# Gated cross-attention with a mixture of biases on one core: the mask's bias added by VectorE, in the operation that takes each head's maximum

## The chip, the core and the metric

The program runs on one core of a Trainium2 chip. A core has engines with queues of their own, which run side by side and wait for each other through semaphores: TensorE (PE in the profile; PEld is its loading of weights), VectorE (DVE), ScalarE (ACT), GpSimd (POOL) and the DMA queue of SyncE (SP). Each engine takes its instructions strictly in the order in which they were issued. TensorE writes its results to PSUM, a small memory of eight banks, from which VectorE and ScalarE fetch them; everything else lies in SBUF.

The metric is the device time of one execution in microseconds (us), as the median of several runs.

## The reference, cut to what matters

There are B = 8 sequences of D = 512 channels and S = 2048 positions. The attention works in patches of W = 128 positions, with H = 8 heads of dh = 32 channels. The mask is one number per position; a key whose mask isn't positive gets a score of -1e9.

```python
q = einsum('ed,bdw->bew', Wq, qp) + bq[:, None]        # qp: layernorm(x), in patches
k = einsum('ed,bdw->bew', Wk, qp) + bk[:, None]
val = einsum('ed,bdw->bew', Wv, vp) + bv[:, None]      # vp: the context, in patches
scores = einsum('bhdi,bhdj->bhij', qh, kh) / sqrt(dh)
scores = where(mp[:, :, None, :] > 0, scores, -1e9)
attn = softmax(scores, axis=-1)
o = gelu(einsum('bhij,bhdj->bhdi', attn, vh))
x = x + tanh(g_xattn) * (einsum('de,bew->bdw', Wo, o) + bo[:, None]) * masks
# then a router over 64 biases: softmax, the 8 largest weights w of each channel's row
x = x + tanh(g_ffn) * (layernorm(x) * sum(w) + w @ expert_bias)
```

## The kernel before, in words

Everything is fp32. The work is cut into 32 chunks of 512 positions (four to a sequence), and each chunk into two pairs of patches, so there are 64 pairs, called `g`. A pair has 16 score matrices of 128 x 128: two patches `i`, and eight heads, numbered by `e` (two halves of the channels) and `r` (four row groups of 32 channels).

The order of the work is written out by hand. The main loop runs over `g` from 0 to 61, and the last two pairs follow with an order of their own. An iteration holds, on each engine's queue, in this order:

- `scores(g)`: TensorE computes the 16 score matrices into four PSUM banks `sc0` to `sc3`, one per row group `r`. For each bank it first issues a product of `negw` with `mneg`, in bf16, which fills the bank with the mask's bias (-1e9 as a sum of three bf16 terms where a key is masked, else 0); the scores are then added onto it in PSUM. Each `sc[r]` is 128 x 512: patch `i`, half `e`, key.
- `weigh(g-2)`: the product of the turned attention weights with the values; ScalarE copies it out (`weighed`).
- `maxima(g, ...)`: VectorE takes the negated maximum of each score row, one `tensor_reduce` of 128 x 512 per bank.
- `exps(g, q)`: ScalarE takes 16 exponentials of 128 x 128 out of PSUM, each with the negated maximum as its bias and the row's sum as a second result. `divide` takes the reciprocals of the sums (VectorE) and multiplies (GpSimd). The weights are turned by TensorE in the next iteration (`turn`), copied by ScalarE (`turned`).
- In an even iteration, from the fifth on: `attend` for two of the four output tiles of a chunk, m = 2 and 3. Its products `po` are emptied by VectorE (L541) and added to the residual by GpSimd (L544). In an odd one: `logits`, whose product `pl` VectorE adds to `lgT` (L591, or L589 for the first of a sequence).
- `queries_and_keys(g // 2 + 1, ...)`: half of the next chunk's queries and keys, by Strassen's scheme in seven block products on TensorE (L374), emptied by VectorE (L381 to L401) with two sums on GpSimd. `between` puts transposes of TensorE between the blocks.
- Statistics of later rows (VectorE), values of the next chunk (`values`, `values_out`), in odd iterations the other two `attend` tiles, and last, from g = 12 on, `mix`: two products `pb`, each added to the output tile by VectorE (L703), which is then stored.

What decides the order between engines around the change is two things. One is VectorE's queue: `maxima` of pair `g` stands behind the two L703 of the iteration before, and ahead of L541 (even) or L591 (odd) and of all that empties the block products. The other is the PSUM banks. `po`, `pl`, `pb` and the block products all take turns in two banks (`ps_mm`, tag `mm`), so each of them can start only when VectorE has emptied the product two before it. In an even iteration the first block product takes the bank that the first `po` has left; in an odd one the third block product (they come two to a bank) takes the bank that `pl` has left. The score banks have one buffer each and are also used by `values` (bank 0) and by the odd `attend` (banks 1 and 2).

The mask's row for a chunk is made by `mask(ch)`, in the middle of each even iteration: `m01` (1/sqrt(dh) for a valid key, 0 for a masked one), which also scales the keys (L401), and `mneg` (1 for a masked key).

Of the kernel before, what the change touches and what calls it, by code (L numbers as in the profile page):

```python
# [8 lines left out]

F32 = mybir.dt.float32  # L10
BF16 = mybir.dt.bfloat16
# [10 lines left out]
def bf16_terms(value, n):  # L22

    import ml_dtypes

    terms = []
    for _ in range(n):
        t = float(ml_dtypes.bfloat16(value))
        terms.append(t)
        value -= t  # L30
    assert value == 0.0
    return terms


@with_exitstack
def flamingo_gated_kernel(
# [23 lines left out]
    nc = tc.nc  # L60
# [37 lines left out]
    raw, xn, cxs, mks, xr = {}, {}, {}, {}, {}  # L98
# [93 lines left out]
    nc.vector.memset(ones, 1.0 / S)  # L192


    negw = const.tile([P, P], BF16, name="negw")
    nc.vector.memset(negw, 0.0)
    terms = bf16_terms(NEG, 3)
    for r in range(HR):
        for i in reversed(range(3)):
            nc.vector.memset(negw[r * DH : r * DH + i + 1, :], terms[i])  # L200

    d1, d2 = slice(0, NM // 2), slice(NM // 2, NM)
# [54 lines left out]
    def statistics(b, m, piece, x_):  # L260

        if b not in st1:
            st1[b] = small.tile([P, NM, S // 512, 6], F32, tag="st1", name=f"st1_{b}")
        nc.vector.bn_stats(st1[b][:, m, piece, :], x_)  # L264
# [41 lines left out]
            nc.gpsimd.tensor_tensor(t4, t2, b21, ALU.subtract)  # L306


    qss, kss, vTs, m01s, mnegs = {}, {}, {}, {}, {}
# [14 lines left out]
    def product(shape, name, r=None):  # L324

        if late:
            late.append(late.pop(0))
            r = late[0]
        if r is not None:
            return ps_sc.tile(shape, F32, tag=f"sc{r}", name=name)  # L330
        return ps_mm.tile(shape, F32, tag="mm", name=name)

    def first_queries_and_keys():


# [90 lines left out]
    def scores(g):  # L426


        ch, h = g // NH, g % NH
        sc = [ps_sc.tile([P, NPP, NE, W], F32, tag=f"sc{r}", name=f"sc_{g}_{r}") for r in range(HR)]  # L430
        rows = [slice(r * DH, (r + 1) * DH) for r in range(HR)]
        bias = mnegs[ch][:, h * HW : (h + 1) * HW].rearrange("p (a w) -> p a w", w=W)
        for r in range(HR):
            nc.tensor.matmul(  # L434
                sc[r], negw[rows[r], :],
                bias[rows[r], :, None, :].to_broadcast([DH, NPP, NE, W]),
                start=True, stop=False,
            )
        for i in range(NPP):
            ws = slice(h * HW + i * W, h * HW + (i + 1) * W)  # L440
            for e in range(NE):
                for r in range(HR):
                    nc.tensor.matmul(  # L443
                        sc[r][:, i, e, :], qss[ch][rows[r], e, ws], kss[ch][rows[r], e, ws],
                        start=False, stop=(i == NPP - 1 and e == NE - 1),
                    )
        nmx = small.tile([P, HR, NPP, NE], F32, tag="nmx", name=f"nmx_{g}")
        at = [work.tile([P, H, W], F32, tag="at", name=f"at_{g}_{i}", bufs=4) for i in range(NPP)]
        rsum = small.tile([P, NPP, H], F32, tag="rsum", name=f"rsum_{g}")
        pairs[g] = {"sc": sc, "nmx": nmx, "at": at, "rsum": rsum, "atT": {}}  # L450

    def maxima(g, rs):
        p = pairs[g]
        for r in rs:
            nc.vector.tensor_reduce(p["nmx"][:, r, :, :], p["sc"][r], AX.X, ALU.max, negate=True)  # L455
# [12 lines left out]

    def divide(g, i, engine=None):
# [276 lines left out]
    for m in range(NM):  # L746
        for j in range(NCH):
            statistics(0, m, j, xr[j][:, m, :])
        ln1[0] = aggregate(st1[0], S // 512, "1_0", m, m + 1)
        shares_of_mean(0, slice(m, m + 1))  # L750
        norm(0, (m,))
        norm(1, (m,))
        if m == NM - 1:
            mask(0)
            weight_sums()
            values_out(0, 0)
            values_out(0, 1)
            values_out(1, 0)
        next(projections)
    st1.pop(0)  # L760
    for k in range(3):
        sums_of_x(1, k)
# [27 lines left out]
    for g in range(NG - NH):  # L790
        ch, h = g // NH, g % NH
        even = h == 0
        nxt = ch + 1
# [138 lines left out]
        if fin == 2:  # L932
            nmean, rs = aggregate(st2.pop(b4), NCH, f"2_{b4}")
# [54 lines left out]
    g = h0 + 1  # L988
# [166 lines left out]
```

## Time and profile before

| what | us |
|---|---|
| median of 3 runs | 1334.58 (1334.14 to 1335.98) |
| the profiled execution | 1334.19 |
| its span | 1332.4 |
| TensorE busy | 1303.9 |
| VectorE busy | 887.1 |
| ScalarE busy | 837.1 |
| GpSimd busy | 794.3 |

"Busy" is the time in which an engine's instructions run; the span is what the profiler saw, some 2 us less than the time of the execution. TensorE's granted clock was 0.997 of full speed. The engine table alone doesn't tell what a change is worth; that is read from the chain of work that ended last, and from the timeline around the change. In the timeline each line has a start, a duration, the engine, the line of the kernel, the operation, output and input tiles, a count, and in brackets how long the engine sat idle before and what ended that. Instructions of one engine overlap a little in the records: the distance from one start to the next is what an instruction costs in its queue, and its duration is somewhat longer.

### The profile page before, as it was taken

What the parts mean: (1) busy time and instruction counts of PE and PEld (TensorE: products, weight loads), DVE (VectorE), ACT (ScalarE), POOL (GpSimd) and SP (SyncE); (2) the same over time, 40 slices, a digit from 0 to 9 for tenths busy, and PEclk for the clock granted to TensorE, in tenths of its full rate; (3) what the DMA queues carried; (4) which work ended last, traced back from release to release, by engine and by line L of the source; (5) the groups of instructions that cost most, each with busy time, mean ns of one, the idle gap of its engine ahead of it and who ended that gap; (6) DMA issues with size and microseconds to landing.
All of it is one profiled execution on the core that took longest, in us unless ns stands there. A gap on an engine that the chain in (4) does not pass through costs nothing.

```text
span 1332.4 us, 26505 instructions
## 1 busy us (share of the span) xinstructions
PE 1303.9 (98%) x9802; PEld 951.6 (71%) x9802; DVE 887.1 (67%) x1815; ACT 837.1 (63%) x2843; POOL 794.3 (60%) x802
## 2 busy tenths in 40 slices
PE   7999999999999999999999999999999999999997
PEld 4777777777777777777777777777777777777653
DVE  5776666576666766677666776667766675666656
ACT  2766765675765765756666665666755666656653
POOL 3655556575566655567655666656566665666642
PEclk9999999999999999999999999999999999999999
DMA  8434223243543443453443453434443423432214
GB/s 282 126 102 126 72 100 128 103 143 101 155 157 120 158 134 104 151 167 124 154 124 115 151 165 118 161 105 130 155 160 120 164 64 112 135 120 79 80 65 174
DMA packets 109729, 173.32 MB, mean 130 GB/s; under 512 B 9248, under 2 KB 43680, under 8 KB 109472
## 3 DMA queue, kind: packets, MB, share of 16 engines
q1 hardware_dynamic: 107536, 168.75, 39.3%
q10 hardware_dynamic: 2064, 2.88, 0.6%
q8 instruction: 77, 1.26, 0.4%
q14 instruction: 52, 0.43, 0.1%
HBM read 138.06 MB, written 33.55 MB: 129 GB/s over the span
## 4 chain that ended last, share of the span: by engine, by line
PE 92%; DVE 3%; DMA 2%; ACT 1%; issue 1%; POOL 0%; SPq 0%; DVEq 0%; ACTq 0%
PE qk L374 27%; PE po L535 17%; PE pv L411 15%; PE pt L487 8%; PE pa L506 5%; PE pb L692 5%; PE pl L573 4%; PE sc L443 4%; PE px L559 4%; PE sc L434 2%; ACT at L464 1%; PE pf L340 1%; DVE st L264 1%; DMA cx<-in_ctx 1%; DVE st L554 1%; PE pg L603 1%
## 5 line engine op out<-in xcount | busy, mean ns | idle before, releaser
L473 POOL TENSOR_TENSOR at<-at,rsum 128x1024 f32<-128x1024 f32 x128 | 244.5, 1910 | 283.3 <-DVE rsum L472 265.6
L464 ACT ACTIVATE at<-sc,nmx 128x128 f32<-128x128 f32 x1024 | 365.7, 415 | 6.0 <-DVE nmx L455 6.0
L464 ACT ACTIVATION_READ_ACCUMULATOR at<-sc,nmx 128x1 f32 x1024 | 260.7, 255 | 0.0
L411 PE MATMUL pv<-wv_sb,cx 128*128 128x256 f32 x1024 | 239.4, 383 | 6.8 <-DMA cx<-in_ctx 6.8
L535 PE MATMUL po<-o,wo_sb 128*128 128x512 f32 x512 | 234.0, 599 | 0.0
L544 POOL TENSOR_TENSOR xr<-t,xr 128x512 f32<-128x512 f32 x124 | 160.5, 1295 | 87.7 <-DVE t L541 86.6
L411 PEld LDWEIGHTS pv<-wv_sb,cx 128*128 128x128 f32 x1024 | 189.4, 192 | 29.3 <-DMA cx<-in_ctx 6.8
L516 ACT COPY o<-pa 128x512 f32<-128x512 f32 x64 | 37.5, 586 | 258.8 <-PE pa L506 258.8
L493 ACT COPY atT<-pt 128x512 f32<-128x512 f32 x256 | 151.6, 623 | 57.2 <-PE pt L487 57.0
L455 DVE TENSOR_REDUCE nmx<-sc 128x4 f32<-128x512 f32 x256 | 158.8, 682 | 12.5 <-PE sc L443 12.5
L535 PEld LDWEIGHTS po<-o,wo_sb 128*128 128x128 f32 x512 | 94.2, 190 | 100.1 <-issue 92.8
L487 PEld LDWEIGHTS pt<-ident,at 128*128 128x128 f32 x1024 | 121.9, 141 | 59.1 <-issue 37.9
L541 DVE SCALAR_TENSOR_TENSOR t<-po,bo_sb,mk 128x512 f32<-128x512 f32 x128 | 95.8, 749 | 100.5 <-PE po L535 99.8
L487 PE MATMUL pt<-ident,at 128*128 128x128 f32 x1024 | 150.6, 275 | 2.8 <-ACT atT L493 2.6
L564 ACT COPY x1T<-px 128x512 f32<-128x512 f32 x120 | 70.3, 586 | 118.3 <-PE px L559 118.2
L374 PE MATMUL qk<-xt,wq_sb 128*128 128x256 f32 x496 | 128.2, 381 | 1.2 <-DVE u L382 1.2
L374 PE MATMUL qk<-xn,wk_sb 128*128 128x256 f32 x496 | 127.6, 380 | 0.1
L374 PE MATMUL qk<-xn,ws 128*128 128x256 f32 x496 | 127.3, 379 | 0.0
L374 PEld LDWEIGHTS qk<-xn,ws 128*128 128x128 f32 x496 | 94.2, 190 | 12.8
L703 DVE TENSOR_TENSOR xr<-pb,xr 128x512 f32<-128x512 f32 x124 | 79.2, 685 | 31.2 <-PE pb L692 31.2
L374 PEld LDWEIGHTS qk<-xn,wk_sb 128*128 128x128 f32 x496 | 89.3, 190 | 10.2 <-DVE lgT L589 0.6
L679 POOL TENSOR_SCALAR xr<-xr,xa,xd 128x512 f32<-128x512 f32 x120 | 94.7, 803 | 0.8
(119 smaller groups left out, 2009.6 us busy)
## 6 DMA issues: line engine op xcount, KB each, us to landing
cx<-in_ctx SPq DMA_DIRECT2D x63, 512.0 KB, 5.3
out_dram<-xr SPq DMA_DIRECT2D x60, 512.0 KB, 3.5
raw<-in_x SPq DMA_DIRECT2D x112, 256.0 KB, 3.4
xn<-in_x SPq DMA_DIRECT2D x28, 1024.0 KB, 7.5
xr<-in_x SPq DMA_DIRECT2D x28, 1024.0 KB, 8.0
mk<-in_mask_Bx1x_ff SPq DMA_DIRECT2D x32, 256.0 KB, 5.4
xr<-in_x SPq DMA_DIRECT2D x10, 256.0 KB, 4.5
out_dram<-xr SPq DMA_DIRECT2D x7, 256.0 KB, 2.5
```

Source lines behind the costliest of these rows:

```text
L374: nc.tensor.matmul(out_, w_[:, j, es], xb[:, j, :], start=(j == 0), stop=(j == NM // 2 - 1))
L411: nc.tensor.matmul(pv[:, i, :], cx[:, m, i * W : (i + 1) * W], wv_sb[:, m, :], start=(m == 0), stop=(m == NM - 1),)
L455: nc.vector.tensor_reduce(p["nmx"][:, r, :, :], p["sc"][r], AX.X, ALU.max, negate=True)
L464: nc.scalar.activation(p["at"][i][:, h, :], p["sc"][r][:, i, e, :], AF.Exp, bias=p["nmx"][:, r, i, e : e + 1], accum_out=p["rsum"][:, i, h ...
L473: (engine or nc.gpsimd).tensor_tensor(p["at"][i], p["at"][i], rs[:, :, None].to_broadcast([P, H, W]), ALU.mult)
L487: nc.tensor.transpose(pt[:, r, :], p["at"][i][:, e * HR + r, :], ident)
L493: nc.scalar.copy(p["atT"][i][:, e * HR : (e + 1) * HR, :], p.pop("pt"))
L535: nc.tensor.matmul(po[:, cs], wo_sb[:, e, m * P : (m + 1) * P], os_[ch][:, e, cs], start=(e == 0), stop=(e == NE - 1),)
L541: nc.vector.scalar_tensor_tensor(t[:, cs], po[:, cs], bo_sb[:, m : m + 1], mks[ch][:, cs], ALU.add, ALU.mult)
L544: (engine or nc.gpsimd).tensor_tensor(xc, t[:, cs], xc, ALU.add)
L679: nc.gpsimd.tensor_scalar(xc, xc, a, d, ALU.mult, ALU.add)
L703: nc.vector.tensor_tensor(xc, pt, xc, ALU.add)
```

## The change

The four bias products of each pair are gone from `scores`, with `negw`, `mneg` and the bf16 terms; each score product now stands alone in its part of the bank. `maxima` becomes 16 operations per pair, one for each patch, `r` and `e`: `tensor_tensor_reduce` reads the 128 x 128 scores from PSUM and the mask's bias row from SBUF, writes the negated sum to the attention tile `at` in SBUF, and writes the minimum of it, which is the negated maximum, to `nmx`. `exps` then works in place on `at`, with a scale of -1. The bias row is made out of `m01` in place by `mask_bias`, once the keys of the chunk have been scaled; so `m01` now has two buffers.

```diff
     def mask(ch):
-        m01 = work.tile([P, CW], F32, tag="m01", name=f"m01_{ch}", bufs=1)
-        nc.vector.tensor_scalar(m01, mks[ch], 0.0, scale, ALU.is_gt, ALU.mult)
-        mneg = work.tile([P, CW], BF16, tag="mneg", name=f"mneg_{ch}")
-        nc.vector.tensor_scalar(mneg, m01, 0.0, None, ALU.is_equal)
-        m01s[ch], mnegs[ch] = m01, mneg
+        m01s[ch] = work.tile([P, CW], F32, tag="m01", name=f"m01_{ch}")
+        nc.vector.tensor_scalar(m01s[ch], mks[ch], 0.0, scale, ALU.is_gt, ALU.mult)
+
+    def mask_bias(ch):
+        nc.vector.tensor_scalar(m01s[ch], m01s[ch], 0.0, NEG, ALU.is_equal, ALU.mult)
...
-        for r in range(HR):
-            nc.tensor.matmul(
-                sc[r], negw[rows[r], :],
-                bias[rows[r], :, None, :].to_broadcast([DH, NPP, NE, W]),
-                start=True, stop=False,
-            )
...
                         sc[r][:, i, e, :], qss[ch][rows[r], e, ws], kss[ch][rows[r], e, ws],
-                        start=False, stop=(i == NPP - 1 and e == NE - 1),
+                        start=True, stop=True,
...
-    def maxima(g, rs):
+    def maxima(g, qs):
         p = pairs[g]
-        for r in rs:
-            nc.vector.tensor_reduce(p["nmx"][:, r, :, :], p["sc"][r], AX.X, ALU.max, negate=True)
+        ch, hf = g // NH, g % NH
+        for q in qs:
+            i = q // 2
+            bias = m01s[ch][:, hf * HW + i * W : hf * HW + (i + 1) * W]
+            for r in (2 * (q % 2), 2 * (q % 2) + 1):
+                for e in range(NE):
+                    nc.vector.tensor_tensor_reduce(
+                        p["at"][i][:, e * HR + r, :], p["sc"][r][:, i, e, :], bias, -1.0, BIG,
+                        ALU.add, ALU.min, p["nmx"][:, r, i, e : e + 1],
+                    )
...
+                at = p["at"][i][:, h, :]
                 nc.scalar.activation(
-                    p["at"][i][:, h, :], p["sc"][r][:, i, e, :], AF.Exp,
-                    bias=p["nmx"][:, r, i, e : e + 1], accum_out=p["rsum"][:, i, h : h + 1],
+                    at, at, AF.Exp, bias=p["nmx"][:, r, i, e : e + 1], scale=-1.0,
+                    accum_out=p["rsum"][:, i, h : h + 1],
                 )
...
         queries_and_keys(nxt, h, between)
+        if not even:
+            mask_bias(nxt)
```

`mask_bias(0)` is called once, after the first chunk's keys.

More of the change, by code (lines that the diff above doesn't have):

```diff
@@ L10 @@
 F32 = mybir.dt.float32
-BF16 = mybir.dt.bfloat16
 AF = mybir.ActivationFunctionType
@@ L19 @@
 NEG = -1e9
[L22 to L32, printed above, removed]
+BIG = 3e38
 @with_exitstack
@@ L192, in flamingo_gated_kernel @@
     nc.vector.memset(ones, 1.0 / S)
-    negw = const.tile([P, P], BF16, name="negw")
-    nc.vector.memset(negw, 0.0)
-    terms = bf16_terms(NEG, 3)
-    for r in range(HR):
-        for i in reversed(range(3)):
-            nc.vector.memset(negw[r * DH : r * DH + i + 1, :], terms[i])
     d1, d2 = slice(0, NM // 2), slice(NM // 2, NM)
@@ L306, in sums_of_x @@
             nc.gpsimd.tensor_tensor(t4, t2, b21, ALU.subtract)
-    qss, kss, vTs, m01s, mnegs = {}, {}, {}, {}, {}
+    qss, kss, vTs, m01s = {}, {}, {}, {}
     def mask(ch):
-        m01 = work.tile([P, CW], F32, tag="m01", name=f"m01_{ch}", bufs=1)
-        nc.vector.tensor_scalar(m01, mks[ch], 0.0, scale, ALU.is_gt, ALU.mult)
-        mneg = work.tile([P, CW], BF16, tag="mneg", name=f"mneg_{ch}")
-        nc.vector.tensor_scalar(mneg, m01, 0.0, None, ALU.is_equal)
-        m01s[ch], mnegs[ch] = m01, mneg
+        m01s[ch] = work.tile([P, CW], F32, tag="m01", name=f"m01_{ch}")
+        nc.vector.tensor_scalar(m01s[ch], mks[ch], 0.0, scale, ALU.is_gt, ALU.mult)
+    def mask_bias(ch):
+        nc.vector.tensor_scalar(m01s[ch], m01s[ch], 0.0, NEG, ALU.is_equal, ALU.mult)
     def new_queries_and_keys(ch):
@@ L431, in scores @@
         rows = [slice(r * DH, (r + 1) * DH) for r in range(HR)]
-        bias = mnegs[ch][:, h * HW : (h + 1) * HW].rearrange("p (a w) -> p a w", w=W)
-        for r in range(HR):
-            nc.tensor.matmul(
-                sc[r], negw[rows[r], :],
-                bias[rows[r], :, None, :].to_broadcast([DH, NPP, NE, W]),
-                start=True, stop=False,
-            )
         for i in range(NPP):
@@ L759, in flamingo_gated_kernel @@
         next(projections)
+    mask_bias(0)
     st1.pop(0)
```

## The prediction, made before the changed kernel was run

> **What bounds the kernel now.** I read the engine table first, then the chain that ended last, then the timeline of one even and one odd iteration, last the waits.
>
> ```profile
> PE 1303.9 (98%) x9802; PEld 951.6 (71%) x9802; DVE 887.1 (67%) x1815; ACT 837.1 (63%) x2843; POOL 794.3 (60%) x802
> PE 92%; DVE 3%; DMA 2%; ACT 1%; issue 1%; POOL 0%; SPq 0%; DVEq 0%; ACTq 0%
> ```
>
> TensorE is the bound: 92% of the chain. Whatever leaves its queue is gained, unless another engine then makes it wait. So the question is whether VectorE, which gets the work, still empties the banks in time. An even iteration (its two queues, 611.9 on):
>
> ```profile
> 611.95 0.39 PE L434 MATMUL sc<-mneg,negw 32*128 32x512 bf16 x4
> 612.18 1.06 PE L443 MATMUL sc<-ks,qs 32*128 32x128 f32 x32
> 613.17 1.08 PE L506 MATMUL pa<-atT,vT 128*32 128x128 f32 x32
> 618.59 1.03 PE L374 MATMUL qk<-xn,wk_sb 128*128 128x256 f32 x4
> ...
> 612.05 1.29 DVE L703 TENSOR_TENSOR xr<-pb,xr 128x512 f32<-128x512 f32 x2 [0.30 <-PE pb L692]
> 613.27 2.48 DVE L455 TENSOR_REDUCE nmx<-sc 128x4 f32<-128x512 f32 x4
> 616.20 0.75 DVE L541 SCALAR_TENSOR_TENSOR t<-po,bo_sb,mk 128x512 f32<-128x512 f32 x1 [0.45 <-PE po L535]
> ```
>
> The block product at 618.59 takes the bank that the L541 of 616.20 leaves (at 616.95). That is 1.64 us in hand, behind maxima of 2.48 us. The odd iteration is tighter: its third block product takes the bank that L591 leaves.
>
> ```profile
> 633.19 2.48 DVE L455 TENSOR_REDUCE nmx<-sc 128x4 f32<-128x512 f32 x4
> 636.08 0.69 DVE L591 TENSOR_TENSOR lgT<-pl,lgT 128x512 f32<-128x512 f32 x1 [0.41 <-PE pl L573]
> ...
> 638.19 1.03 PE L374 MATMUL qk<-xn,wk_sb 128*128 128x256 f32 x4
> ```
>
> L591 ends at 636.77, 1.42 us early. That this wait is real is seen where VectorE happened to be late (an input came late at 114):
>
> ```profile
> 115.44 2.46 DVE L455 TENSOR_REDUCE nmx<-sc 128x4 f32<-128x512 f32 x4
> 117.83 0.68 DVE L589 COPY lgT<-pl 128x512 f32<-128x512 f32 x1
> 118.56 0.73 PEld L374 LDWEIGHTS qk<-xn,wk_sb 128*128 128x128 f32 x4 [0.55 <-DVE lgT L589]
> 119.53 1.03 PE L374 MATMUL qk<-xn,ws 128*128 128x256 f32 x4
> ```
>
> The product starts 0.05 us after L589's end (118.51), and the next four matmuls follow after 0.97 us instead of the 0.87 of undisturbed blocks: a wait costs 0.1 more than itself.
>
> **The change, part by part.**
>
> *Bias products gone.* Start to start, 611.95 to 612.18, they hold TensorE for 0.23 us a pair; 64 pairs give 14.7 us, and that is all that can be gained. The chain books 0.33 us a pair, with modelled ends; I take the starts. Below: the scores' first weight load (186 ns) lay under these products and may now show, which would leave 0.1.
>
> *Sixteen operations for four.* The old four cost 0.60 us each, start to start. The new one does not occur in the trace. Its main part is like L703 (PSUM and SBUF in, SBUF out): start to start 0.61 us at 512 columns, and L381 against L589 (422 ns at 256 columns, 691 at 512) gives 1.05 ns a column, so 128 columns cost 0.61 - 384 x 0.00105 = 0.21 us. How the minimum gets out is open. From below: with the main part, at no cost, T = 0.21. ScalarE's exponentials need an instruction of their own for their sums, ACTIVATION_READ_ACCUMULATOR, 0.09 us start to start (615.06 to 615.15). VectorE's shortest instruction in the trace, MATCH_VALUE_LOAD, takes 0.07. From above: each main part runs to its end before the read, 0.28 us (L591 on 128x128: 280 ns) plus 0.07, T = 0.35. I take 0.21 + 0.07, T = 0.28 us, since short neighbours on VectorE do overlap (MATCH_VALUE_LOAD and MATCH_REPLACE8 follow each other at 0.20 us a couple, with 80 and 208 ns). Sixteen cost 4.48 us against 2.4.
>
> [...]
>
> *What waits behind them.* Even: L541, then the bank for the first block. The operations start where L455 did, 613.27, since L703 stands in front and depends on `pb`, not on the scores. New: 613.27 + 4.48 + 0.75 + 0.05 = 618.55, while TensorE would come at 618.59 - 0.23 = 618.36. It waits, 0.1 more for the restart: 618.65, which is 0.06 later than before. Odd: 633.19 + 4.48 + 0.69 + 0.05 + 0.10 = 638.51 against 638.19, 0.32 later. The next buffers in line are not late: between these waits and the block product that needs VectorE's following results lie two blocks (1.73 us) and a turn (0.44), and VectorE needs 1.1 to 2.4 us for its L541, mask, reciprocal and two L381/L382 operations.
>
> *Mask.* `mneg` goes: 1.30 us mean in each even iteration, behind L541 (its 0.43 at 63.5 shows that the rest is waiting for GpSimd). `mask_bias` (like L313, 0.42 us) comes in odd iterations behind L401, where GpSimd waits for the reciprocal (1.29 us idle at 644.86) and VectorE idles about 1 us before each L541 later (649.19, 650.91). At nothing; if that cover were gone, 31 x 0.42 = 13 us.
>
> *Exponentials from SBUF, in place.* L628 (64 columns, SBUF) steps at 0.24 us before its read, L464 (128 columns, PSUM) at 0.255; with 64 columns more (0.05) the new one costs some 0.29, 0.04 more each, 0.6 us a pair. ScalarE idles 4.0 us a pair before L516 alone (258.8 us in 64); hidden. Uncovered: 41 us. It follows VectorE at 0.385 against 0.28, so it isn't held up. Score banks come free earlier; nothing waited for that.
>
> *Sum.* L703 stands in front in the iterations 13 to 61: 25 odd x 0.32 + 24 even x 0.06 = 9.4 us. In the other 15 pairs VectorE has slack (L455 idles 1.25 to 1.35 us for the scores and can now start on the first ones), and the gain stays: 15 x 0.2 = 3. Net +6.4: 1334.2 (the profiled execution, 0.4 below the median) becomes 1340.6; I say 1341. 10 ns in T are 16 x 0.01 x 49 = 8 us: T decides, and break-even lies near 0.272.
>
> **Rivals.**
>
> 1. *Faster: VectorE stays in time.* If T is below (637.96 - 633.19 - 0.74) / 16 = 0.252, neither wait arises and 0.22 us a pair is gained: 1320. From 0.252 to 0.268 part of it: up to 1331. For it: the 0.07 for the read is an instruction of eight columns, and one value may cost less. Against: it needs the gain of 0.23 whole.
> 2. *Each short operation runs to its end,* T = 0.35: 5.60 us. Odd 638.19 to 639.63, even 618.59 to 619.77: 25 x 1.44 + 24 x 1.18 = 64, nothing gained elsewhere: 1398. For it: the read depends on the main part just in front. Against: ScalarE's read starts 0.255 us after its main part began, where that runs 0.37. [...] The trace disagrees for plain operations (L703's two start 0.61 us apart and run 0.68).
> 3. *The products cost less than they seem:* the weight load shows and 0.1 of 0.23 is gained. Where TensorE waits anyway, nothing changes; elsewhere at most 0.13 a pair is lost, 15 + 24 pairs, 5 us: 1346 with T = 0.28.
> 4. *ScalarE's cover is gone:* the 41 us show as waits of turns for their copies: some 1375. Against: the idle time named.
>
> **How the numbers follow.** Forecast (T 0.268 to 0.32, with 3 beside it): 0.44, 1332 to 1372. Rival 1: 0.35. Rival 2 and what lies between: 0.17. Rival 4: 0.04. About 0.2%, 2.7 us, is what a measurement can tell from no change; T from 0.268 to 0.276 falls into that, 0.12, and the top of rival 1 a little. Faster 0.33, same 0.13, slower 0.54. Range 1320 to 1385: rival 1 whole, and rival 2 up to T = 0.335. Around the forecast alone: 1332 to 1372.
>
> **What would show it.** Bias products: the distance from the last `pb` to L506 falls from 1.22 to 1.0 us. T: sixteen operations over their total; a row of accumulator reads beside them. Waits: TensorE idle before L374 on L541 (even) and L591 (odd), 25 times and 0.1 to 0.5 us. ScalarE: L464's row without reads rising. Wrong if TensorE waits at `sc`, `pt` or `px` instead, or if T is below 0.25 or above 0.32.

## The result, and the profile after

The median is 1330.36 us (1328.9 to 1331.36, 6 runs) against 1334.29 us for the kernel before in the same comparison: a ratio of 0.9971, with a 95% interval of 0.9961 to 0.9981. The kernel is 0.3% faster. The forecast was 1341 and slower; the time lies inside its range, near the side that was given to rival 1. The profiled execution took 1330.44 us, its span is 1328.6 us at a granted clock of 0.997.

The engine table and the shares of the chain, as the page of the kernel after has them:

```profile
PE 1296.8 (98%) x9546; PEld 944.2 (71%) x9546; DVE 915.4 (69%) x3594; ACT 871.4 (66%) x2843; POOL 791.8 (60%) x802
PE 91%; DVE 4%; ACT 2%; DMA 2%; issue 1%; POOL 0%; SPq 0%; DVEq 0%; ACTq 0%
```

TensorE has 256 matmuls fewer and is busy 7.1 us less, half of the 14.7 that the removed products held its queue. VectorE is busy 28 us more, ScalarE 34; each has one more per cent of the chain.

The costliest groups of the new work (line, engine, operation, output and inputs, shape and count; then busy us and mean ns of one; then idle time before):

```profile
L447 ACT ACTIVATE at<-at,nmx 128x128 f32<-128x128 f32 x1024 | 396.4, 392 | 4.9 <-DVE nmx L435 4.9
...
L435 DVE CUSTOM_DVE_ANT_0 at<-sc,m 128x128 f32<-128x128 f32 x1024 | 220.7, 285 | 11.2 <-PE sc L416 11.2
...
L435 DVE DVE_READ_ACCUMULATOR2_ANT nmx<- 128x1 f32 x1024 | 84.7, 83 | 0.0
```

So the minimum is fetched by an instruction of its own, 1024 of them, 83 ns each. What that costs is not in this table but in the timeline. One even and one odd iteration, both queues (start, duration, engine, line, operation):

```profile
610.83 1.17 PE L416 MATMUL sc<-ks,qs 32*128 32x128 f32 x32
611.93 1.08 PE L489 MATMUL pa<-atT,vT 128*32 128x128 f32 x32
617.36 1.03 PE L354 MATMUL qk<-xn,wk_sb 128*128 128x256 f32 x4
...
612.14 0.28 DVE L435 CUSTOM_DVE_ANT_0 at<-sc,m 128x128 f32<-128x128 f32 x1
612.34 0.08 DVE L435 DVE_READ_ACCUMULATOR2_ANT nmx<- 128x1 f32 x1
612.34 0.28 DVE L435 CUSTOM_DVE_ANT_0 at<-sc,m 128x128 f32<-128x128 f32 x1
...
615.51 0.75 DVE L524 SCALAR_TENSOR_TENSOR t<-po,bo_sb,mk 128x512 f32<-128x512 f32 x1
...
635.32 0.68 DVE L574 TENSOR_TENSOR lgT<-pl,lgT 128x512 f32<-128x512 f32 x1
...
636.84 1.03 PE L354 MATMUL qk<-xn,wk_sb 128*128 128x256 f32 x4
```

Three readings. From the scores to the attention products it is 610.83 to 611.93, 1.10 us; before it was 1.22 with the bias products: 0.12 gained, not 0.23. The sixteen operations take 612.14 to 615.51, 3.37 us, so T = 0.21: the read starts together with the next operation (both at 612.34) and takes next to nothing from the queue. And neither product waits: L574 ends at 636.00 and its product comes at 636.84, L524 ends at 616.26 and its product comes at 617.36. Less 0.05 for the handing over, VectorE has 0.79 us in hand in odd iterations and 1.05 in even ones.

Where the kernel gives time back shows in the first pairs (first the product that waits, then VectorE ahead of it):

```profile
42.42 1.13 PE L354 MATMUL qk<-xt,wq_sb 128*128 128x256 f32 x4 [0.94 <-DVE u L362]
120.22 1.13 PE L354 MATMUL qk<-xn,wk_sb 128*128 128x256 f32 x4 [1.21 <-DVE lgT L572]
...
41.50 0.41 DVE L361 COPY s<-qk 128x256 f32<-128x256 f32 x1
41.94 0.42 DVE L362 TENSOR_TENSOR u<-qk,s 128x256 f32<-128x256 f32 x1
...
119.47 0.69 DVE L572 COPY lgT<-pl 128x512 f32<-128x512 f32 x1
```

L361 follows directly on the last new operation of pair 0, L572 on that of pair 5. There VectorE has nothing in hand, and 3.37 us in place of 2.4 lie on the path whole: 0.97 us each.

The starts of the scores in every pair, read off the timelines, put this into one table (differences to the kernel before, us; a negative number is earlier). Between pair 6 and pair 61 every single iteration of the kernel after is 0.11 to 0.13 us shorter.

| kernel | pair 0 | pair 1 | pair 6 | pair 61 | pair 63 | span |
|---|---|---|---|---|---|---|
| before (its own times) | 35.61 | 43.95 | 131.28 | 1235.02 | 1264.90 | 1332.4 |
| after | +0.30 | +1.26 | +1.65 | -4.67 | -4.24 | -3.8 |

Had all 63 steps gained 0.115, the last pair would stand at -7.2. The account of the 3.4 us that are missing in the span: 0.30 at the start (not put down to the change, see below), 2.04 in the pairs 0 to 5, 0.66 in the last two steps, where the product `po` waits 0.4 us for ScalarE's gelu, and 0.44 behind the last scores, where TensorE waits 0.94 and 2.09 us instead of 0.81 and 1.81. Of the 2.04, the pairs 0 and 5 lose 1.07 and 1.06 and pair 2 loses 0.24; pair 1 gives 0.35 back.

The start goes with the granted clock. The scores of pair 0 began between 35.1 and 36.0 us in eleven of the fifteen executions profiled here, and between 37.3 and 37.5 in the other four (`products_back`, `short_products`, `five_apart` and `one_later` below). In just these four TensorE is granted half its clock for 3.4 us from some 26 us on. One window in the kernel after and in `short_products` (its length, busy us and instructions of PE, PEld, DVE, ACT and POOL, granted clock, DMA share, GB/s):

```profile
26.00:30.00 4.00, 4.00 (x10) 1.71 (x9) 3.90 (x9) 1.52 (x2) 3.17 (x11) 1.00 0.14 14
26.00:30.00 4.00, 4.00 (x6) 1.52 (x5) 3.90 (x9) 1.52 (x2) 3.15 (x11) 0.57 0.13 20
```

### The profile page after: what moved, and what is told of

It is laid out like the page before. It is cut to its first block, busy times and chain, and to the rows that moved or that the text cites. A ratio compares the mean times of both kernels' runs of the same rounds, so it can differ in the third digit from the quotient of the medians.

```text
span 1328.6 us, 27774 instructions
## 1 busy us (share of the span) xinstructions
PE 1296.8 (98%) x9546; PEld 944.2 (71%) x9546; DVE 915.4 (69%) x3594; ACT 871.4 (66%) x2843; POOL 791.8 (60%) x802
## 4 chain that ended last, share of the span: by engine, by line
PE 91%; DVE 4%; ACT 2%; DMA 2%; issue 1%; POOL 0%; SPq 0%; DVEq 0%; ACTq 0%
PE qk L354 27%; PE po L518 17%; PE pv L391 15%; PE pt L470 8%; PE sc L416 5%; PE pa L489 5%; PE pb L675 5%; PE pl L556 4%; PE px L542 4%; ACT at L447 1%; PE pf L321 1%; DVE st L243 1%; DMA cx<-in_ctx 1%; DVE at L435 1%; DVE st L537 1%
## 5 line engine op out<-in xcount | busy, mean ns | idle before, releaser
L447 ACT ACTIVATE at<-at,nmx 128x128 f32<-128x128 f32 x1024 | 396.4, 392 | 4.9 <-DVE nmx L435 4.9
L435 DVE CUSTOM_DVE_ANT_0 at<-sc,m 128x128 f32<-128x128 f32 x1024 | 220.7, 285 | 11.2 <-PE sc L416 11.2
L447 ACT ACTIVATION_READ_ACCUMULATOR at<-at,nmx 128x1 f32 x1024 | 195.4, 191 | 0.0
L499 ACT COPY o<-pa 128x512 f32<-128x512 f32 x64 | 37.5, 586 | 238.7 <-PE pa L489 238.7
L476 ACT COPY atT<-pt 128x512 f32<-128x512 f32 x256 | 141.8, 576 | 54.6 <-PE pt L470 54.4
L524 DVE SCALAR_TENSOR_TENSOR t<-po,bo_sb,mk 128x512 f32<-128x512 f32 x128 | 95.6, 748 | 67.4 <-PE po L518 66.7
L416 PEld LDWEIGHTS sc<-ks,qs 32*128 32x128 f32 x2048 | 64.7, 186 | 49.6 <-DVE t L524 21.1
```

The lines of the kernel that those rows point to most:

```text
L416: nc.tensor.matmul(sc[r][:, i, e, :], qss[ch][rows[r], e, ws], kss[ch][rows[r], e, ws], start=True, stop=True,)
L435: nc.vector.tensor_tensor_reduce(p["at"][i][:, e * HR + r, :], p["sc"][r][:, i, e, :], bias, -1.0, BIG, ALU.add, ALU.min, p["nmx"][:, r, i ...
L447: nc.scalar.activation(at, at, AF.Exp, bias=p["nmx"][:, r, i, e : e + 1], scale=-1.0, accum_out=p["rsum"][:, i, h : h + 1],)
L476: nc.scalar.copy(p["atT"][i][:, e * HR : (e + 1) * HR, :], p.pop("pt"))
L524: nc.vector.scalar_tensor_tensor(t[:, cs], po[:, cs], bo_sb[:, m : m + 1], mks[ch][:, cs], ALU.add, ALU.mult)
```

## The experiments

Each time below stands beside the kernel before on the same chip in the same comparison: 1334.18, 1333.88, 1334.18 and 1333.71 us in the four of them. "Base" names the kernel that was edited.

**The products alone.** Base: before. Scores of masked keys stay without their bias.

```diff
-        for r in range(HR):
-            nc.tensor.matmul(
-                sc[r], negw[rows[r], :],
-                bias[rows[r], :, None, :].to_broadcast([DH, NPP, NE, W]),
-                start=True, stop=False,
-            )
...
-                        start=False, stop=(i == NPP - 1 and e == NE - 1),
+                        start=True, stop=True,
```

> The kernel before with the four bias products per pair left out (the mask's bias is missing; every other instruction as before, with the four reductions of 128x512 from PSUM). Theory A (a product pass hides the first weight load of the scores, so only the part beyond it is gained): from one score block to the next 0.11 to 0.12 us less, scores from their first start to the next product 1.10 us, in all 64 x 0.115 = 7 us less than before, 1327. Rival (the products cost their full 0.23 us, and VectorE's new operations ate half of it in the changed kernel): 0.23 us a pair, 14 us less, 1320.

Measured: 1327.12 us (1325.82 to 1328.3), ratio 0.9948 (0.9934 to 0.9961). The scores of pair 61 come 6.81 us earlier, in steps of 0.11 to 0.13 from pair 6 on; the pairs 0 to 5 together gain 0.52. One block of scores and the attention products behind it:

```profile
707.87 1.17 PE L436 MATMUL sc<-ks,qs 32*128 32x128 f32 x32
708.97 1.08 PE L499 MATMUL pa<-atT,vT 128*32 128x128 f32 x32
```

Theory A holds: the block takes 1.10 us as in the kernel after, and without the products a pair is 0.115 us shorter, 7 us in all. The 0.23 between the starts was not the worth of the products.

**The products put back.** Base: after. Products of zeros with the old shape ahead of the scores.

```diff
+        for r in range(HR):
+            nc.tensor.matmul(
+                sc[r], negw[rows[r], :],
+                zeros[rows[r], None, None, :].to_broadcast([DH, NPP, NE, W]),
+                start=True, stop=False,
+            )
...
-                        start=True, stop=True,
+                        start=False, stop=(i == NPP - 1 and e == NE - 1),
```

> The changed kernel with four products of zeros put in front of the scores of each pair, of the old shape (bf16, 128x512 per bank), scores added onto them. Theory A: 0.115 us a pair more than the changed kernel, +7 us, 1337, that is some 3 us slower than before: that rest is what the new operations on VectorE and ScalarE cost by themselves, in the first iterations, in the sixth and at the end. Rival (0.23 us a product pass): +14 us, 1344.

Measured: 1337.75 us (1336.21 to 1339.28), ratio 1.0025 (1.0014 to 1.0036). Theory A again. Sharper than the time: the difference to the kernel before is 3.82 us at pair 6 and 3.82 us at pair 61, with steps of 0.00 or 0.01 between. So in the steady iterations the sixteen operations, the reads, `mask_bias` and the longer exponentials cost nothing that shows, and what they cost lies in the first six pairs (2.15 us, of which some 0.6 come with an input that landed later in pair 5) and in the last two steps (0.67). The rest of the 3.6 us of span is the clock: the window at half clock near 26 us puts the first scores 1.67 later, and the end, without such a window, is 0.85 shorter.

**The products twice.** Base: before, a second round of them (masked scores get -2e9).

```diff
-        for r in range(HR):
...
-                start=True, stop=False,
+        for k in range(2):
+            for r in range(HR):
...
+                    start=(k == 0), stop=False,
```

> The kernel before with eight of the mask's bias products a pair instead of four (the second four add the bias once more, so scores of masked columns get -2e9). Theory A (the first round also hides the scores' weight load of 0.19 us, so that taking it away yielded only 0.115 us a pair; a further round has nothing to hide and costs all of its stream, the 0.23 us between L434's and L443's starts): 64 x 0.23 = 14.7 us, 1348 against 1334. Rival (a round of these products costs 0.115 us by itself, the 0.23 between the starts is not all stream): 64 x 0.115 = 7.4 us, 1341.

Measured: 1346.36 us (1345.52 to 1348.15), ratio 1.0096 (1.0082 to 1.011), 12.5 us over the kernel before. In the steady iterations the second round costs 0.21 to 0.22 us. Its timeline:

```profile
617.30 0.61 PE L435 MATMUL sc<-mneg,negw 32*128 32x512 bf16 x8
617.75 1.06 PE L444 MATMUL sc<-ks,qs 32*128 32x128 f32 x32
618.73 1.08 PE L507 MATMUL pa<-atT,vT 128*32 128x128 f32 x32
```

From the bias products to the scores it is now 0.45 us, and from scores to attention products 0.98. The first round thus takes its 0.23 as it seems to, and the second 0.215. What vanishes with the first round is half regained by something that it had covered: in the kernel after, the weight load of the first scores and their first matmul are both recorded from 610.83 on, while before the load of 186 ns lay under the bias products: it starts at 611.96, and the first score product at 612.18. Here the load thus ran beside the products that stand ahead of it in TensorE's queue: it started 0.01 us behind the first of them and 0.22 ahead of the score product. The single records show where the time comes back: from the first score product of a row group to its second it is 0.21 us in the kernel after and 0.11 in the kernel before; between later ones it is 0.11 in both.

**Short products.** Base: after. Four bf16 products of zeros, 128 columns each.

```diff
+        for r in range(HR):
+            nc.tensor.matmul(
+                sc[r][:, 0, 0, :], negw[rows[r], :], zeros[rows[r], :], start=True, stop=False
+            )
...
-                        start=True, stop=True,
+                        start=(i + e > 0), stop=True,
```

> The kernel after with four products of zeros (bf16, 128 columns each, a quarter of the old length) ahead of the scores in every pair. If what the old products hid is the scores' weight load and they hid it by their length, a short stream hides little of it: four of 128 columns at the old products' rate are 0.06 us, beside about 0.09 for their own load's share, and the time grows by 0.05 to 0.1 us a pair: 3 to 6 us, 1333 to 1336. Rival (any product ahead hides the whole load, whatever its length): the 0.115 us come back less 0.06 to 0.075: 0.04 to 0.055 a pair, 2.5 to 3.5 us faster, 1327 to 1328.

Measured: 1331.58 us (1331.31 to 1333.47), ratio 0.9987 (0.9979 to 0.9996): between the two, and both expectations miss. Its first scores came 1.6 us later than in the kernel after (the half clock at 26 us), so the steady steps say more: 0.10 us below before, 0.013 above after.

```profile
613.25 0.23 PE L419 MATMUL sc<-zeros,negw 32*128 32x128 bf16 x4
613.32 1.12 PE L426 MATMUL sc<-ks,qs 32*128 32x128 f32 x32
614.36 1.08 PE L499 MATMUL pa<-atT,vT 128*32 128x128 f32 x32
```

The short round takes 0.07 us between the starts and adds only 0.013 to the pair: 0.06 of it lies under time that passes anyway. Put together, what a pair spends ahead of its scores is 0.115 us with no product, 0.128 with 128 columns, 0.23 with 512 and 0.445 with 1024. That is close to the larger of two things side by side, a load that shows with about 0.115 and the stream of the products, and far from their sum (0.185 for 128 columns, where 0.128 was measured). Here the stream of 128 columns hid 0.06 us of the load, nearly the 0.07 that it lasts itself, and that of 512 columns the whole 0.115.

**Three of the operations done again, in place.** Base: after.

```diff
+MORE = [(0, 0, 1), (1, 3, 0), (2, 1, 1)]
...
-                    nc.vector.tensor_tensor_reduce(
+                    for _ in range(2 if (q, r, e) in MORE else 1):
+                      nc.vector.tensor_tensor_reduce(
```

> The changed kernel with 3 of the 16 operations per pair issued twice (0.63 us more of VectorE per pair). Theory B (VectorE's time counts only beyond the slack in front of the block products, 0.79 us in an odd iteration and 1.05 in an even one): no wait in the steady iterations; only where a wait is there already (pairs 0, 1 and 5) 0.63 us each, +2 us, 1332. Rival (the operations are on the path): 64 x 0.63 = +40 us, 1370.

Measured: 1345.07 us (1343.86 to 1348.52), ratio 1.0088 (1.0073 to 1.0102). A miss by 13 us. The timeline tells why:

```profile
622.24 0.29 DVE L437 CUSTOM_DVE_ANT_0 at<-sc,m 128x128 f32<-128x128 f32 x1
622.45 0.08 DVE L437 DVE_READ_ACCUMULATOR2_ANT nmx<- 128x1 f32 x1
622.56 0.29 DVE L437 CUSTOM_DVE_ANT_0 at<-sc,m 128x128 f32<-128x128 f32 x1
622.78 0.08 DVE L437 DVE_READ_ACCUMULATOR2_ANT nmx<- 128x1 f32 x1
622.78 0.29 DVE L437 CUSTOM_DVE_ANT_0 at<-sc,m 128x128 f32<-128x128 f32 x1
```

The repeat (622.56) writes what the operation just ahead writes, and starts 0.32 after it instead of 0.21. Three of them cost 1.0 us, not 0.63, and 1.0 is over the odd slack of 0.79. The trace also tells what holds the repeat: it alone carries a wait for VectorE's own semaphore, which the read ahead of it raises at its end (622.53), and it starts 0.03 later. So it is a wait in the program, not the operation. The experiment did not measure what it was made for; it was repeated as follows.

**Three, and five, done again into a place of their own.** Base: after.

```diff
+    twin = const.tile([P, W], F32, name="twin")
+    twinm = const.tile([P, 1], F32, name="twinm")
...
+                    if (q, r, e) in MORE:
+                        nc.vector.tensor_tensor_reduce(
+                            twin, p["sc"][r][:, i, e, :], bias, -1.0, BIG,
+                            ALU.add, ALU.min, twinm,
+                        )
```

> The kernel after with 3 of the 16 new operations of each pair done a second time right behind the first, but into an output of their own, so that nothing is overwritten by the next operation. Theory B (an operation more costs VectorE's queue 0.21 us, and TensorE loses nothing until the emptying of lgT ends 0.79 us later): 0.63 us more a pair, below the slack, so the steady iterations keep their period of 19.81 and 19.88 us, and only the three early pairs that wait already lose up to 0.6 us each: 1331 to 1333. Rival (the loss of the earlier run with three repeats, 14.7 us, came from the operations themselves, by VectorE's hold on the banks or by the exponentials behind them): 1340 or more again.

> As the run with three, but 5 of the 16 operations of each pair are done a second time into an output of their own. Theory B: 1.03 us more a pair, 0.24 beyond the odd iterations' 0.79, with 0.10 for the restart 0.34 in 25 of them, 8.5 us; the even iterations' 1.05 just holds; the early pairs 3 us: about 1342 (1338 to 1346), with waits of TensorE on lgT. If the even slack is used up too, another 24 x 0.1: 1344. Rival (no threshold, each operation costs the same share as in the run with eight repeats, 15 us an operation): 1400.

Measured with three: 1332.74 us (1331.22 to 1333.98), ratio 0.999 (0.9981 to 0.9999). From pair 6 to the end the steps differ from those of the kernel after by 0.00 to 0.03 us; 2.3 of the 2.4 us were lost in the pairs 0 to 5. With five: 1349.56 us (1346.87 to 1351.32), ratio 1.0112 (1.0099 to 1.0126), above the 1342 expected, since the first six pairs lost 7.3 us instead of 3 and the even slack is used up too. (In the profiled execution two windows of 3.4 us at half clock, from 56.2 and 127.8 us on, fall into these pairs.) The steps from pair 13 on are what theory B says: five times 0.21 is 1.055, of which the odd iterations hold 0.79 and the even ones 1.05, and with 0.10 for the restart this gives 0.37 and 0.105. Measured are 0.37 to 0.39 (0.44 in the iterations of a sequence's first logits) and 0.10 to 0.12. One odd iteration of the kernel with five:

```profile
651.44 1.13 PE L357 MATMUL qk<-xn,wk_sb 128*128 128x256 f32 x4
652.41 1.03 PE L357 MATMUL qk<-xn,ws 128*128 128x256 f32 x4
...
650.70 0.69 DVE L582 TENSOR_TENSOR lgT<-pl,lgT 128x512 f32<-128x512 f32 x1
```

L582 ends at 651.39 and the product starts 0.05 later; the four after it follow at 0.97 us, not 0.87. The wait is the one that the prediction named, place, handing over and restart included. It has a threshold: in the steady iterations three operations more are free, five are not.

**Eight done again, in place.** Base: after.

```diff
+MORE = [(0, 0, 0), (0, 1, 0), (1, 2, 0), (1, 3, 0), (2, 0, 0), (2, 1, 0), (3, 2, 0), (3, 3, 0)]
...
+                    for _ in range(2 if (q, r, e) in MORE else 1):
```

> The changed kernel with 8 of the 16 operations per pair issued twice (1.68 us more of VectorE per pair, as if one operation took 0.32 us). Theory B: odd iterations wait 1.68 - 0.79 + 0.10 for the restart = 0.99 us at the third block product, even ones 1.68 - 1.05 + 0.10 = 0.73 us at the first; 25 x 0.99 + 24 x 0.73 = 42, with the early iterations some 50 us more than the changed kernel, 1380. Rival (on the path): 64 x 1.68 = +108. Rival (VectorE still has room, it is 69% busy): within 5 us of the changed kernel.

Measured: 1453.85 us (1452.4 to 1457.33), ratio 1.09 (1.0885 to 1.0915), 74 us over the 1380 expected. The expectation used 0.21 for a repeat; with the 0.33 that they take in place, 2.6 us a pair, the odd iterations lose 1.9 and the even ones 1.65, 87 us. The starts of the scores account for the whole loss of the profiled execution, 126.9 us of span: 23.3 in the pairs 0 to 5, into which 20 us at half clock fall, 11.5 in the pairs 6 to 12, 89.8 in the pairs 13 to 60 (2.0 and 1.73 a pair) and 3.4 in the last two steps, less 1.1 ahead of the first scores and behind the last. The waits of TensorE (releaser, us in all, times, longest) show both predicted places:

```profile
PE qk L355 <- DVE t L526: 42.3, 29, 2.4
PE qk L355 <- DVE lgT L576: 36.0, 21, 1.7
PE qk L355 <- DVE lgT L574: 16.1, 8, 3.5
```

**Additions without the minimum, and exponentials without the bias.** Base: after. The first leaves out the maxima and the shift by them, the second computes the maxima but leaves out the shift.

```diff
-                    nc.vector.tensor_tensor_reduce(
-                        p["at"][i][:, e * HR + r, :], p["sc"][r][:, i, e, :], bias, -1.0, BIG,
-                        ALU.add, ALU.min, p["nmx"][:, r, i, e : e + 1],
+                    nc.vector.tensor_tensor(
+                        p["at"][i][:, e * HR + r, :], p["sc"][r][:, i, e, :], bias, ALU.add
```

```diff
-                    at, at, AF.Exp, bias=p["nmx"][:, r, i, e : e + 1], scale=-1.0,
+                    at, at, AF.Exp, scale=-1.0,
```

> The kernel after with plain additions in place of the operations that also take a minimum: no maxima, no reads of the accumulator, and exponentials without the shift by the maximum (the maxima are left out). Theory (the accumulator's read of 83 ns runs beside the next operation's start and costs the queue nothing): sixteen operations still take 3.3 to 3.4 us from first start to last end, a step of 0.20 to 0.21 us, and the time is within 2 us of the kernel after, 1329 to 1332; the waits of the first pairs stay. Rival (the read or the accumulation holds the queue for part of it, 0.03 us of the step or more): the sixteen take 2.9 us or less, the waits at the pairs 0, 1 and 5 shrink by about 0.5 us each, 1328 or less, with ScalarE unchanged.

> The kernel after with its maxima as they are, but the exponentials take no bias (the shift by the maximum is left out). In the run with plain additions the exponentials fell from 392 to 300 ns and the time by 4 us, all of it in the pairs 1, 3, 5 and at the end, none in the steady iterations. If those were ScalarE's (its exponentials reach the attention products and the gelu late): the exponentials step at 0.29 us again, the wait at the last pair (0.43 us lost against before) turns into a gain, the pairs 1 and 3 gain as there: 1326 to 1328. If they were VectorE's (maxima shorter by 0.12 us a pair): 1330, as the kernel after.

Measured without the minimum: 1326.25 us (1325.07 to 1326.7), ratio 0.9943 (0.993 to 0.9957); without the bias alone: 1327.43 us (1326.21 to 1328.98), ratio 0.9951 (0.9937 to 0.9965). The sixteen additions of the first one with the operation behind them, and the exponentials of the second one, from its groups:

```profile
609.90 3.25 DVE L435 TENSOR_TENSOR at<-sc,m 128x128 f32<-128x128 f32 x16
613.07 0.74 DVE L523 SCALAR_TENSOR_TENSOR t<-po,bo_sb,mk 128x512 f32<-128x512 f32 x1
...
L447 ACT ACTIVATE at<-at 128x128 f32<-128x128 f32 x1024 | 301.5, 300 | 6.0 <-DVE nmx L435 6.0
```

The sixteen plain additions take 3.17 us to the start of what follows, the sixteen with the minimum 3.37: a step of 0.198 against 0.211. So the minimum costs 0.013 of a step, read and all, and in the steady iterations both kernels have the very period of the kernel after (steps of -0.01 to +0.01). The time forecast for the additions was nevertheless missed by 3 us; it fell into the rival's range, though the rival's condition, sixteen in 2.9 us, did not hold. The second kernel tells where most of the 3 us come from: with VectorE's queue as in the kernel after, it gains 0.72 us in the pairs 1 to 3, 0.35 in pair 5, and 0.54 in the last two steps, and its span is 3.0 us shorter; most of the rest lies behind the last scores, where TensorE waits 0.57 and 1.34 us instead of 0.94 and 2.09 for the last pair's tiles. Without the bias an exponential steps at 0.29 us instead of 0.385, and these parts are put down to ScalarE, all but the one in pair 5: there VectorE starts its operations 0.35 us sooner after the scores, since it waits 1.82 us for an input's transfer (`raw`) instead of 2.24. Pair 0 doesn't move (+0.01): that part is VectorE's. The additions shorten it by 0.21, their sixteen steps of 0.013. (The profiled execution of the additions lies 1.2 us below their median; it has no window at half clock near the end.) Neither kernel is a version to use, since a softmax without its shift isn't safe for every input.

**Half of the operations later.** Base: after. Three kernels issue the second eight operations (and their exponentials) later: in odd iterations from pair 3 on behind the logits' copies (`odd_later`); there and in pair 0 behind the first emptying (`one_later`); there and in the pairs 0 and 1 (`half_later`).

```diff
-        maxima(g, (2, 3))
+        late_half = not even and g > 1
+        if not late_half:
+            maxima(g, (2, 3))
...
+            if g > 1:
+                maxima(g, (2, 3))
             exps(g, 2)
             exps(g, 3)
```

> The kernel after with the second eight of the new operations (and their exponentials) issued later: in the odd iterations from pair 3 on behind the logits' copies, in the pairs 0 and 1 behind the first emptying of the projections' bank. Theory (the kernel after loses about 1 us each in the pairs 1 and 5 and 0.8 in another early pair to VectorE's longer maxima, and nothing in the steady iterations): those waits go, the attention products then wait for the later exponentials a little in those pairs, net -1 to -3 us, 1327.5 to 1329.5, and the steady odd iterations keep their period unless ScalarE's later exponentials reach TensorE. Rival (the early waits come from the input's transfers and not from VectorE's queue, or the exponentials become late instead): no change or slower, 1330 or more.

> The kernel after with the second eight of the new operations and their exponentials issued behind the first emptying of the projections' bank in pair 0 alone, and behind the logits' copies in the odd iterations from pair 3 on; pair 1 keeps the order of the kernel after. Expected from the starts of the scores: pair 0 costs no longer than before the change (1.0 us less than after), pair 1 as before or as after (in the run with both early pairs moved it lost 1.2 us more because its attention waited for the later exponentials), pair 5 0.9 to 1.2 us less than after: -1 to -2.5 us, 1328 to 1329.5. Rival: pair 1 makes up for what pair 0 gained, and only pair 5 is left: -1 us or less, 1329.5 to 1330.5.

> The kernel after with the second eight of the new operations behind the logits' copies in the odd iterations from pair 3 on, and nothing else moved. Expected: pair 5 loses its 0.95 to 1.2 us, all others stay: -1.0 us against the kernel after, 1329.3. Rival (the later exponentials of the steady odd iterations cost something over the whole run): 1330.4 or more.

Measured: `half_later` 1329.65 us (1328.5 to 1332.74), ratio 0.9971 (0.9962 to 0.9981); `one_later` 1331.12 (1329.68 to 1331.33), 0.9973 (0.9963 to 0.9984); `odd_later` 1330.09 (1328.91 to 1330.48), 0.9968 (0.9955 to 0.998). None can be told from the kernel after, and the times expected, 1329.5 or less, were missed by 0.2 to 1.6 us. The steps can: pair 5 gets 0.92 to 1.2 us shorter in all three, its wait of 1.21 us for L572 is gone, and no steady iteration gets longer, so its loss was VectorE's queue. Pair 0 gets 1.2 shorter where its half is moved, and pair 1 gives 1.7 back: the attention weights of pair 0 then come late (in `half_later` TensorE waits 1.01 and 1.93 us for them).

`odd_later` has its last scores 0.87 us earlier than the kernel after and ends at the same time. The windows show where that went. TensorE waits some 2 us for the last pair's weights, and in or behind that wait it is granted half its clock for a while. Busy time by windows, first of the kernel after, then of `odd_later` (window, its length, busy us and instructions of each engine, granted clock, DMA share, GB/s):

```profile
1272.00:1273.00 1.00, 1.00 (x33) 0.70 (x32) 0.00 (x0) 0.92 (x2) 1.00 (x1) 0.90 0.09 29
1273.00:1274.00 1.00, 1.00 (x10) 0.30 (x4) 0.00 (x0) 0.99 (x2) 1.00 (x3) 0.50 0.20 10
...
1276.00:1277.00 1.00, 1.00 (x8) 0.44 (x5) 0.32 (x1) 0.00 (x0) 0.16 (x1) 0.89 0.98 381
```

```profile
1268.00:1271.00 3.00, 0.92 (x7) 0.68 (x6) 1.66 (x4) 2.44 (x12) 1.82 (x2) 0.71 0.40 152
1271.00:1272.00 1.00, 1.00 (x15) 0.64 (x17) 0.00 (x0) 0.36 (x1) 1.00 (x1) 0.50 0.22 76
...
1275.00:1276.00 1.00, 1.00 (x4) 0.24 (x2) 0.00 (x0) 0.07 (x1) 0.28 (x1) 0.50 1.01 395
1276.00:1277.00 1.00, 1.00 (x8) 0.43 (x5) 0.31 (x1) 0.00 (x0) 0.00 (x0) 0.97 0.08 29
```

A mean between 1.00 and 0.50 tells how much of a window ran at half clock: in the kernel after 0.2 us of 1272 to 1273, then all up to 1276, then 0.2 us, 3.4 us in all; in `odd_later` 1.7 us before 1271, then all up to 1276, 6.8 us in all, twice as long. In the kernel before it is 3.4 us from 1275.6 to 1279.0. In `products_back`, with the same wait of 2.09 us at 1278.1 to 1280.2, it is none:

```profile
1278.00:1280.00 2.00, 0.12 (x2) 0.00 (x0) 0.89 (x4) 2.00 (x11) 0.91 (x1) 1.00 0.24 90
1280.00:1283.00 3.00, 2.80 (x42) 1.66 (x44) 0.48 (x1) 2.23 (x4) 2.91 (x3) 1.00 0.55 130
```

In these traces the clock stayed at half for 3.41 us (the kernel before and the one after) or for twice that (`odd_later`). What sets it off they don't show. In the 3.41 us ahead of the halving TensorE sat idle for 1.97 us in the kernel after, 1.76 in `odd_later` and 2.48 in the kernel before. In `products_back` it sat idle for 0.67 + 2.09 = 2.76 of the 3.41 us up to 1280.2, more than in any of these, and the clock up to 1283 is 1.00; so the idle time alone doesn't decide it. Another 3.41 us at half clock are, by estimate, at most 1.7 us of lost work (the eight logits products behind it take 3.34 us in the kernel after, 3.0 of them at half clock, and 1.87 in `products_back`); in `odd_later` TensorE waits through the first 1.26 us of its 6.8, which leaves (3.41 - 1.26) / 2 = 1.1, about the 0.87 gained.

## Why the prediction was wrong, point by point

**T = 0.21 + 0.07 was the step that failed first.** The main part was right: 0.21, from L703 and the price of a column. The read exists: 1024 of them, 83 ns each. That there would be one was the author's estimate before the run, by ScalarE's exponentials, which need one. The 0.07 for it is shown by no run: the read runs beside the next operation, and with the minimum itself it adds 0.013 to the step. The end "at no cost", which the prediction named as its lower bound, was the true one. Both neighbours that the prediction reasoned from do hold their queues, ScalarE's read for 0.09 us and VectorE's MATCH_VALUE_LOAD, from which the 0.07 was taken, for 0.07 from its start to that of MATCH_REPLACE8; VectorE's read doesn't. With T = 0.21 the condition of rival 1 (T below 0.252) was met, and no steady iteration waits.

**0.23 us a pair for the products was the second.** The prediction named the doubt itself (a weight load of 186 ns that "may now show, which would leave 0.1") and carried it as rival 3, but worked its sum with 0.2 or 0.22. It is 0.115, as two runs show from two sides, products taken out and put back; the run with the products doubled shows that their stream does take 0.215, so that the missing half is what they covered. The direction of the error is opposite to the first: that the time came within 1% of the forecast is luck.

**The waits had the right place and the right size.** L541 and L591 (now L524 and L574) are what TensorE would wait for, and the 0.05 for the handing over and 0.10 for the restart are in the traces. With the measured gain the odd iterations begin to wait at a T of 0.21 + 0.79 / 16 = 0.259; the run with three operations more stays below it, that with five goes over it and loses what the slack doesn't hold.

**"In the other 15 pairs VectorE has slack" was wrong for two of them.** In pair 0 and pair 5 VectorE's queue had nothing in hand, and each loses the whole difference of 3.37 and 2.4 us. Pair 5 is the very place (at 115 to 119 us) that the prediction showed to prove the wait real; it was not then counted as a loss.

**ScalarE's exponentials** step at 0.385 us, the 0.04 more that were forecast, and are hidden in the steady iterations (the steps with the products put back differ by 0.00). The cover ends at the edges: in the first pairs and the last, where TensorE waits for them or for the gelu behind them. `mask_bias` costs nothing in the steady iterations.

**The rivals.** Rival 1 gave the condition that came true, but a time of 1320. From there to what was measured: 64 x (0.22 - 0.115) = 6.7 us that the products are not worth, and 3.4 us given back at both ends, 1330.1. Rival 2 is refuted (T = 0.35): operations of 285 ns start every 0.21 us. Only the repeats in place, at 0.32, waited for the end of the read ahead of them, and those by a wait in the program. Rival 3 was right in its premise and wrong in its price, since it kept T = 0.28. Rival 4 shows only at the edges: at most the 3 us that exponentials without a bias get back, not 41.

## What to carry to other kernels

Time between two starts on the bound engine is not yet gain: ask what the removed work covered (here a weight load), and count the longer of the two, not their sum (0.128 us were measured for 0.07 of products beside a load of 0.115). Where a short step decides and the trace doesn't have the operation, both ends of its cost are forecasts of their own; here a helper instruction's price said little of another one's, on the same engine too (MATCH_VALUE_LOAD holds VectorE's queue for 0.07 us, the read and the minimum together for 0.013). And count edges by themselves: here the steady iterations, with 0.79 and 1.05 us in hand, hid the new work (steps of 0.00 or 0.01 with the products put back), while the pairs 0 and 5, where VectorE had nothing in hand, paid 0.97 us each, and the last two steps lost 0.67.

## What the runs showed of the hardware beyond that

- In `three_more` an operation that writes the same output as the one directly ahead started 0.32 us after it, with different outputs 0.21. A wait in the program held it: it started 0.03 us after the read ahead of it had raised VectorE's semaphore.
- An exponential of 128x128 in SBUF took 392 ns with a bias per partition (the kernel after) and 300 ns without one (`plain_exps`), 92 less; its step fell from 0.385 to 0.29 us. The read of the sum held ScalarE's queue for 0.09 us in both.
- One wait of some 2 us near the end came with half the granted clock for 0 us (`products_back`), 3.4 (the kernel after, and with 1.81 us of wait the kernel before) or 6.8 (`odd_later`): by estimate, half of each, up to 1.7 us of lost work for each 3.4, in which a small gain ahead of it can disappear. What decides between them wasn't shown. Four of the fifteen profiled executions had 3.4 us of half clock ahead of the first scores, from some 26 us on, and started them at 37.3 to 37.5 us, the other eleven at 35.1 to 36.0.
